# A cross-attention block in float32: half of the W1 product by seven block products, a re-ordered W2 sum, and the second norm's statistics at another place

## The chip, the cores and the metric

The kernel runs on one core of a Trainium2 chip. The metric is the device time of one execution in microseconds (us), lower is better. A core has a matrix engine (PE, whose weight loads are listed as PEld), a vector engine (DVE), an activation engine (ACT), a general engine (POOL) and a queue engine that issues transfers (SP). Each engine works through its own list of instructions in order, and they meet at semaphores.

## The reference

There are 128 batch rows of 128 tokens with 256 features; everything is float32.

```python
q = (x @ Wq + bq), k = (c @ Wk + bk), v = (c @ Wv + bv)       # 16 heads of 16 features
scores = einsum('bhqd,bhkd->bhqk', q, k) / 4
scores = where(j < i, scores, -1e30)                          # strictly earlier keys only
attn = softmax(scores); attn[:, :, 0, :] = 0
ctx = einsum('bhqk,bhkd->bhqd', attn, v)
x1 = layer_norm(x + ctx @ Wo + bo, g1, b1_ln)
out = layer_norm(x1 + relu(x1 @ W1 + b1) @ W2 + b2, g2, b2_ln)   # W1: 256 x 1024, W2: 1024 x 256
```

## The kernel before

Two batch rows at a time (a "pair", 256 tokens) go through the block; there are 64 pairs. The order of the instructions on every engine is written out by hand: the functions are called in the order in which the engines are to have the work, and no planner changes it. From pair 7 on, `step(p)` is the loop's body. It works on several pairs at once, each at another stage:

- pair p: scores (`scores_both`), mask, exponential, sums and normalisation, values, and the turn of the probabilities (`turn` on DVE, then `bring`, 16 transfers issued by SP);
- pair p + 1: queries and keys; pair p + 2: tokens transposed on DVE (`tokens`);
- pair p - 2: probabilities times values (`weigh`, `context`), output product, first sum, its statistics (`attention_stats`) and `norm1`;
- pair p - 3: `residual1` on POOL, and the W1 product with its Relu (`hidden`), eight feature blocks of 128 as float32 products of 128 x 128 weights and 256 tokens; the program's one product becomes two passes on PE;
- pair p - 4: the W2 product by seven block products (`second_by_seven`), with the combinations of the hidden tile formed on POOL (`combine_hidden`, a step's first POOL work) and of W2 once (`combine_w2`); the seven results, in two banks `py` and `pz`, are added to the residual `x1b` on DVE (`sum_of_seven`, lines L823 and L831), and the second norm's statistics follow at the step's end (`stats` on DVE, `scale_and_shift` on POOL);
- pair p - 5: `norm2` on ACT, `finish` on POOL, `store`.

The product by seven is the Winograd form: a 2 x 2 block product takes seven block products instead of eight, and more additions. Its sum in the kernel before, with t of four blocks:

```python
        add(t, x1b, 0)
        add(t[:, 1:], t[:, 1:], 1)
        add(t[:, 2:], t[:, 2:], 2)
        add(t[:, 1::2], t[:, 1::2], 3)
        nc.vector.tensor_tensor(
            t[:, :3], t[:, :3], pz[:, : 3 * P].rearrange("p (n d) -> p n d", d=P), ALU.add
        )
```

PE's order in a step is: L483/L493 (`weigh`), L376 (scores), L261 (queries), L512 (output product), L261 (keys), L301 (values), L794 (W2 by seven), L699 (W1). DVE's is: masks (L390, L743) and maxima (L747, L754), first sum (L538) and its statistics (L525, L526), softmax sums (L421, L422), turn of x1 (L663), tokens (L247), first probability turn (L436), `sum_of_seven`, two more turns (L436), the second norm's statistics (L525, L526). ACT has `context` (L505), the exponentials (L762), queries (L272), `norm1` (L554), keys (L291), values (L311, L316), `norm2` (L591) and the Relus (L707).

Every product's result lies in one of eight PSUM banks. The scores take banks 6, 7, 4, 5 (low half) and 0 to 3 (high half); queries 4, output product 5, keys 0, values 1, py 6, pz and the context product 7; the W1 product takes 2, 3, 4, 0. `empty(n)` puts n empty instructions into PE's list; `second_by_seven` has one behind each of its seven products, and pair 1's W1 product (`hidden`, outside the loop) has two or three behind each product.

Work tiles come from pools: a tile of the same tag takes the slot of an older one when that one's readers are done. `hT` and `hS` have one slot each, `t2` two.

Of the kernel before, what the change touches and what calls it, by code (L numbers as in the profile page):

```python
# [8 lines left out]
F32 = mybir.dt.float32  # L9
# [10 lines left out]
def tile_cross_attention_block(  # L20
# [104 lines left out]
    load_tokens(0, slice(0, 2))  # L125
    wk = weight(Wk, "wk")
    wq = weight(Wq, "wq")
    c_first = const.tile([P, 4, D], F32, tag="c_first", name="c_first")
    nc.scalar.dma_start(c_first[:, 0:2], c[0:2].rearrange("b p d -> p b d"))
    bk_c = column(bk, "bk_c")  # L130
    bq_c = column(bq, "bq_c")
# [78 lines left out]
    def at_bank(i, name):  # L210
        return psum.tile([P, 512], F32, tag=f"b{i}", name=name)
# [39 lines left out]
    def add_bo(p):  # L251
        st = states[p]
        st["xb"] = proj.tile([P, 2, D], F32, tag="xb", name=f"xb_{p}")
        nc.gpsimd.tensor_tensor(
            st["xb"], tokens_of[p // 2][:, p % 2 * 2 : p % 2 * 2 + 2], bov_r[:, None, :].to_broadcast([P, 2, D]), ALU.add
        )
# [47 lines left out]
                )  # L304

    def values_out(p):
        st = states[p]
        pv = st.pop("pv")
        st["vz"], st["vd"] = vzs[p % 2], vds[p % 2]
        for s in range(2):  # L310
            nc.scalar.copy(  # L311
                st["vz"][:, s, :, 0:4:3, :],
                pv[:, s * D : (s + 1) * D].rearrange("p (r e d) -> p r e d", e=2, d=DK),
            )
        for e in range(2):
# [69 lines left out]
    def mask(p, hi, rs):  # L385
        st = states[p]
        n = P if hi else HP
        no = neg.rearrange("p u j -> p (u j)") if hi else neg[:, 1, :]
        for r in rs:
            nc.vector.tensor_tensor(  # L390
                st["sm", hi][:, 4 * r : 4 * r + 4, :],
                st["sps", hi][r][:, : 4 * n].rearrange("p (n j) -> p n j", j=n),
                no[:, None, :].to_broadcast([P, 4, n]),
                ALU.add,
            )
# [185 lines left out]
    def scale_and_shift(p):  # L581

        st = states[p]
        deviation(p, 2)
        shift(p, 2)
# [199 lines left out]
    def second_by_seven(p):  # L785

        st = states[p]
        hT, hs = st["hT"], st["hS"]
        py = st["py"] = at_bank(6, f"py_{p}")
        pz = st["pz"] = at_bank(7, f"pz_{p}")  # L790

        def product(out, left, right, after):
            for k in range(FC // 2):
                nc.tensor.matmul(  # L794
                    out, left(k), right(k), start=(k == 0), stop=(k == FC // 2 - 1)
                )
                empty(after // (FC // 2) + (after % (FC // 2) > k))

        def raw(e, s):
            return lambda k: hT[:, 2 * k + e, s * P : (s + 1) * P]  # L800

        def weights(e, h):
            return lambda k: w2[:, 2 * k + e, h * P : (h + 1) * P]

        product(py[:, :P], raw(0, 0), weights(0, 0), 1)
        product(pz[:, :P], raw(1, 0), weights(1, 0), 1)
        product(pz[:, 2 * P : 3 * P], raw(1, 1), lambda k: wt[:, 3, k], 1)
        product(py[:, 3 * P :], lambda k: hs[:, 0, k], lambda k: wt[:, 0, k], 1)
        product(py[:, 2 * P : 3 * P], lambda k: hs[:, 2, k], lambda k: wt[:, 2, k], 1)
        product(py[:, P : 2 * P], lambda k: hs[:, 1, k], lambda k: wt[:, 1, k], 1)  # L810
        product(pz[:, P : 2 * P], lambda k: hs[:, 3, k], weights(1, 1), 1)

    def sum_of_seven(p):

        st = states[p]
        t2 = st["t2"] = ffn.tile([P, 2, D], F32, tag="t2", name=f"t2_{p}")
        t = t2.rearrange("p s (h d) -> p (s h) d", h=2)
        py, pz = st.pop("py"), st.pop("pz")
        x1b = st.pop("x1b").rearrange("p s (h d) -> p (s h) d", h=2)

        def add(to, of, at):
            n = to.shape[1]
            nc.vector.tensor_tensor(  # L823
                to, of, py[:, None, at * P : (at + 1) * P].to_broadcast([P, n, P]), ALU.add
# [6 lines that stand above are left out]
        nc.vector.tensor_tensor(  # L831
            t[:, :3], t[:, :3], pz[:, : 3 * P].rearrange("p (n d) -> p n d", d=P), ALU.add
        )

    def second_half(p, s):

# [331 lines left out]
    def sixth(p):  # L1168

        weigh(p - 2)  # L1170
        context(p - 2)
        scores_both(p)
        add_bo(p - 1)
        mask(p, 0, B)
# [36 lines left out]

    def step(p):
        last = p == NP - 1
        weigh(p - 2)
        context(p - 2)
        scores_both(p)
        if p == 7:
            norm2(p - 6)
        combine_hidden(p - 4, POOL_ALONE)
        if p == 7:  # L1220
            finish(p - 6)
            store(p - 6)
        add_bo(p - 1)
        load_ahead(p)
        mask(p, 0, B)
        if last:
            mask(p, 0, A)
        mask_high(p, A)
        exponential_by_head(p, 1, ONES)
        mask_high(p, B)  # L1230
        exponential_by_head(p, 1, TWOS)
        if not last:
            mask(p, 0, A)
        low_maximum(p)
        exponential_by_head(p, 0, range(H))
        if not last:
# [134 lines left out]
```

## Time and profile before

| | us |
|---|---|
| median of three runs | 1527.93 (1526.05 to 1528.2) |
| the profiled execution | 1528.67 |
| its span in the profile | 1527.0 |
| PE busy | 1514.3 (99%) |
| DVE busy | 1332.4 (87%) |
| POOL busy | 1255.9 (82%) |
| ACT busy | 1118.3 (73%) |

The median and the profiled execution are whole device times; the span runs from the first to the last instruction that the profiler recorded. Times within the trace are us from the span's start. A group's row gives the busy time, the mean duration in ns, and the idle time of its engine just before it with what ended most of it; a timeline's row gives start, duration, engine, line, operation and, in brackets, the idle time before it. PE's idle time means little by itself, as its ends are modelled; starts are measured.

### The profile page before, as it was taken

How to read it: one execution, taken by the hardware profiler on the slowest of the kernel's cores; microseconds unless marked ns; L12 is line 12 of the kernel's file. 1: busy time of each engine (PE TensorE's matmuls, PEld its weight loads, DVE VectorE, ACT ScalarE, POOL GpSimd, SP SyncE). 2: the span in 40 equal slices, each digit the busy share in tenths (PEclk: the TensorE clock that was granted, in tenths of full speed). 3: DMA queues.
4: the chain of work that ended last, by engine and by line, in shares of the span. 5: the costliest groups of instructions: out<-in, count | busy, mean ns of one | idle time of the engine just before them, and what ended most of it. 6: DMA issues, size and time to landing. Idle time of an engine off the chain costs nothing.

```text
span 1527.0 us, 47892 instructions
## 1 busy us (share of the span) xinstructions
PE 1514.3 (99%) x17926; PEld 1360.6 (89%) x17926; DVE 1332.4 (87%) x2498; ACT 1118.3 (73%) x3391; POOL 1255.9 (82%) x1282
## 2 busy tenths in 40 slices
PE   8999999999999999999999999999999999999998
PEld 7788998998989989989989899899899898998997
DVE  7989988988988988889889889889898898898885
ACT  5668777877877877778778778777777787787752
POOL 6876988888888888888888888888888888888883
PEclk9999999999999999999999999999999999999999
DMA  9356665555656656655556666566566566564441
GB/s 192 87 120 141 154 156 132 135 136 132 143 139 138 143 120 141 148 132 135 137 134 142 145 134 136 132 136 148 134 136 138 128 141 147 133 144 109 115 112 49
DMA packets 415285, 204.24 MB, mean 134 GB/s; under 512 B 282448, under 2 KB 383056, under 8 KB 415056
## 3 DMA queue, kind: packets, MB, share of 16 engines
q1 hardware_dynamic: 412768, 199.34, 56.7%
q8 instruction: 144, 2.36, 0.7%
q10 hardware_dynamic: 2288, 1.85, 0.5%
q14 instruction: 85, 0.70, 0.2%
HBM read 70.26 MB, written 33.29 MB: 68 GB/s over the span
## 4 chain that ended last, share of the span: by engine, by line
PE 94%; DVE 3%; POOL 1%; DMA 1%; issue 1%; ACT 0%; SPq 0%; POOLq 0%; DVEq 0%
PE ph L699 28%; PE py L794 14%; PE pz L794 10%; PE pq L261 7%; PE po L512 7%; PE pv L301 7%; PE pk L261 7%; PE pss L376 6%; PE pc L493 4%; PE pc L483 2%; DVE tb L436 1%; PE py L719 0%; DMA x1t<-tbx 0%; DVE sm L390 0%; DVE su L421 0%
## 5 line engine op out<-in xcount | busy, mean ns | idle before, releaser
L699 PE MATMUL ph<-x1T,w 128*128 128x256 f32 x2048 | 453.6, 380 | 0.7 <-DMA x1T<-x1t 0.7
L699 PEld LDWEIGHTS ph<-x1T,w 128*128 128x128 f32 x2048 | 385.0, 190 | 50.9 <-issue 1.2
L423 POOL TENSOR_TENSOR sm<-sm,rs 128x1024 f32<-128x1024 f32 x192 | 359.3, 1898 | 3.9 <-DVE rs L422 3.3
L762 ACT ACTIVATE sm<-pss,nmx 128x128 f32<-128x128 f32 x944 | 249.9, 414 | 127.3 <-DMA pT<-tb 81.0
L707 ACT ACTIVATE hT<-ph,b1e_c 128x256 f32<-128x256 f32 x504 | 209.1, 467 | 171.3 <-PE ph L699 161.3
L762 ACT ACTIVATE sm<-sm,nmx 128x64 f32<-128x64 f32 x944 | 232.2, 337 | 5.1 <-DVE nmx L754 0.3
L421 DVE TENSOR_REDUCE su<-sm 128x8 f32<-128x1024 f32 (+1 forms) x192 | 225.8, 1176 | 4.0 <-ACT sm L409 3.8
L436 DVE STREAM_TRANSPOSE tb<-sm 128x1024 f32<-128x1024 f32 x186 | 221.0, 1214 | 0.0
L390 DVE TENSOR_TENSOR sm<-pss,neg 128x256 f32<-128x256 f32 (+1 forms) x276 | 108.2, 435 | 121.2 <-PE pss L376 115.4
L532 POOL TENSOR_SCALAR ve<-mv 128x2 f32<-128x2 f32 x127 | 28.7, 226 | 191.7 <-DVE mv L526 190.9
L794 PE MATMUL py<-wt,hS 128*128 128x128 f32 x1440 | 170.6, 275 | 0.0
L794 PEld LDWEIGHTS py<-wt,hS 128*128 128x128 f32 x1440 | 165.7, 192 | 0.0
L747 DVE TENSOR_REDUCE nmx<-pss 128x4 f32<-128x512 f32 x236 | 150.8, 680 | 0.0
L261 PE MATMUL pq<-xT,wq 128*128 128x256 f32 x504 | 125.5, 392 | 0.5 <-DVE sm L390 0.5
L291 ACT ACTIVATE kT<-pk,bkh,half 128x256 f32<-128x256 f32 x252 | 120.3, 558 | 4.0 <-PE pk L261 4.0
L512 PE MATMUL po<-wo,cxT 128*128 128x256 f32 x512 | 121.3, 380 | 0.7 <-ACT cxT L505 0.7
L301 PE MATMUL pv<-wv,cT 128*128 128x256 f32 x512 | 121.0, 380 | 0.0
L261 PE MATMUL pk<-cT,wk 128*128 128x256 f32 x504 | 119.2, 380 | 0.0
L512 PEld LDWEIGHTS po<-wo,cxT 128*128 128x128 f32 x512 | 97.1, 190 | 14.3 <-ACT cxT L505 1.2
L261 PEld LDWEIGHTS pq<-xT,wq 128*128 128x128 f32 x504 | 90.9, 190 | 20.8 <-issue 9.6
L301 PEld LDWEIGHTS pv<-wv,cT 128*128 128x128 f32 x512 | 97.4, 190 | 13.0
L261 PEld LDWEIGHTS pk<-cT,wk 128*128 128x128 f32 x504 | 95.9, 190 | 13.0 <-issue 0.2
(135 smaller groups left out, 2966.6 us busy)
## 6 DMA issues: line engine op xcount, KB each, us to landing
pT<-tb SPq DMA_DIRECT2D x976, 96.0 KB
x1t<-tbx SPq DMA_DIRECT2D x252, 64.0 KB
x1T<-x1t SPq DMA_DIRECT2D x63, 256.0 KB
out_dram<-t SPq DMA_DIRECT2D x63, 256.0 KB
xb<-in_x_dram SPq DMA_DIRECT2D x124, 128.0 KB
cb<-in_ctx_dram SPq DMA_DIRECT2D x124, 128.0 KB
x<-in_x_dram SPq DMA_DIRECT2D x31, 512.0 KB
w<-in_L_xattn_W_dram SPq DMA_DIRECT2D x2, 1024.0 KB
```

What stands on the lines that cost most here:

```text
L261: nc.tensor.matmul(ps[:, m * TP : (m + 1) * TP], w[:, k, m * P : (m + 1) * P], src[:, k, :], start=(k == 0), stop=(k == KC - 1),)
L291: nc.scalar.activation(st["kT"][:, m, e, :], pk[:, m * TP : (m + 1) * TP], AF.Identity, bias=bkh[:, m, e : e + 1], scale=half[:, e : e + 1],)
L301: nc.tensor.matmul(pv[:, s * D : (s + 1) * D], st["cT"][:, k, s * P : (s + 1) * P], wv[:, k, :], start=(k == 0), stop=(k == KC - 1),)
L421: nc.vector.tensor_reduce(su, sm[:, part, :], AX.X, ALU.add)
L423: nc.gpsimd.tensor_tensor(sm[:, part, :], sm[:, part, :], rs[:, :, None].to_broadcast([P, part.stop - part.start, n]), ALU.mult,)
L436: nc.vector.transpose(st["tb"][:, :, at : at + 256].rearrange("p j (n a) -> p n j a", a=32), st["sm", hi].rearrange("p h j -> p (h j)")[:, ...
L512: nc.tensor.matmul(po[:, s * D : (s + 1) * D], cxT[:, k, s, :], wo[:, k, :], start=(k == 0), stop=(k == KC - 1),)
L699: nc.tensor.matmul(ph[:, i * TP : (i + 1) * TP].rearrange("p (s i a) -> p s i a", s=2, a=32), w1[:, k, (f + i) * P : (f + i + 1) * P], st[ ...
L707: nc.scalar.activation(st["hT"][:, f + i, :], ph[:, i * TP : (i + 1) * TP], AF.Relu, bias=(b1e_c if p else b1_c)[:, f + i : f + i + 1], sc ...
L747: nc.vector.tensor_reduce(st["nmx", 1][:, 4 * r : 4 * r + 4], st["sps", 1][r].rearrange("p (n j) -> p n j", j=P), AX.X, ALU.max, negate=True,)
L762: nc.scalar.activation(sm[:, h, :], src, AF.Exp, bias=nmx[:, h : h + 1], scale=1.0)
L794: nc.tensor.matmul(out, left(k), right(k), start=(k == 0), stop=(k == FC // 2 - 1))
```

## The change

Blocks 0 to 3 of the eight W1 feature blocks are formed as two 2 x 2 block products (NI = 2) by seven products each; blocks 4 to 7 stay as they were, one bank each. The combinations of W1 are formed once on POOL (`combine_w1`, in `sixth`), those of x1 in each step on POOL (`combine_normed`), and the seven results are put together in the hidden tile: one copy on ACT (`keep`), five adds on DVE (`u2`, `u3`, `rest`), and then a Relu from SBUF to SBUF. The W2 sum becomes one copy on ACT (`keep_first`) and six adds on DVE (`sum_of_products`). The second norm's statistics of a pair move from the end of its step to behind `low_maximum` of the next step, and `norm2` moves to behind `rest`. Each of the first six W2 products gets 7 empty instructions for 1, the last 6: 48 in a step for 7. The first context tile gives its own storage up and shares the slots of the context blocks. `sum_of_seven` and `hidden` stay in use behind the loop.

```diff
-    c_first = const.tile([P, 4, D], F32, tag="c_first", name="c_first")
+    c_first = loads.tile([P, 4, D], F32, tag="cb2", name="c_first", bufs=2)
...
-        product(py[:, :P], raw(0, 0), weights(0, 0), 1)
+        product(py[:, :P], raw(0, 0), weights(0, 0), 7)
...
+    def combine_normed(p):
+        st = states[p]
+        x1T = st["x1T"]
+        xs = st["xS"] = ffn.tile([P, 4, NS, 32], F32, tag="xS", name=f"xS_{p}", bufs=1)
+        nc.gpsimd.tensor_tensor(xs[:, 0], x1T[:, 1, :, 0, :], x1T[:, 1, :, 1, :], ALU.add)
+        nc.gpsimd.tensor_tensor(xs[:, 2], x1T[:, 0, :, 0, :], x1T[:, 1, :, 0, :], ALU.subtract)
+        nc.gpsimd.tensor_tensor(xs[:, 1], xs[:, 0], x1T[:, 0, :, 0, :], ALU.subtract)
+        nc.gpsimd.tensor_tensor(xs[:, 3], x1T[:, 0, :, 1, :], xs[:, 1], ALU.subtract)
+
+    class Hidden:
+        WHERE = {1: (2, 0), 6: (2, 1), 7: (3, 0), 4: (3, 1), 2: (4, 0), 3: (4, 1), 5: (5, 0)}
...
+        def run(self, which):
...
+            ps = self.of(which)
+            for i in range(NI):
+                nc.tensor.matmul(
+                    ps[:, i * P : (i + 1) * P].rearrange("p (n a) -> p n a", a=32),
+                    left(i), right, start=True, stop=True,
+                )
+        def keep(self):
+            nc.scalar.copy(self.h[:, 0, 0], self.one(1))
+        def u2(self):
+            nc.vector.tensor_tensor(self.h[:, 1, 0], self.h[:, 0, 0], self.one(6), ALU.add)
+        def u3(self):
+            nc.vector.tensor_tensor(self.h[:, 1, 1], self.h[:, 1, 0], self.one(7), ALU.add)
+            nc.vector.tensor_tensor(self.h[:, 0, 1], self.h[:, 1, 1], self.one(4), ALU.add)
+        def rest(self):
+            odd = self.hT[:, 1 : 2 * NI : 2].rearrange("p i (s t) -> p i s t", s=2)
+            nc.vector.tensor_tensor(
+                odd, odd, self.one(5)[:, :, None, :].to_broadcast([P, NI, 2, P]), ALU.add
+            )
+            low = self.h[:, :, 0]
+            nc.vector.tensor_tensor(
+                low, low, self.of(2, 2).rearrange("p (e i t) -> p e i t", e=2, i=NI), ALU.add
+            )
+        def relu(self, f):
+            nc.scalar.activation(
+                self.hT[:, f], self.plains.get(f, self.hT[:, f]), AF.Relu,
+                bias=b1e_c[:, f : f + 1], scale=1.0,
+            )
...
+    def sum_of_products(p):
...
+        add(u[:, 1], u[:, 0], py[:, P : 2 * P])
+        add(u[:, 2], u[:, 1], py[:, 2 * P : 3 * P])
+        add(t[:, :3], x1b[:, :3], u)
+        add(t[:, 3], x1b[:, 3], u[:, 2])
+        add(t[:, 1::2], t[:, 1::2], py[:, None, 3 * P :].to_broadcast([P, 2, P]))
+        add(t[:, :3], t[:, :3], pz[:, : 3 * P].rearrange("p (n d) -> p n d", d=P))
...
         low_maximum(p)
+        if p > 7:
+            second_stats(p - 5)
         exponential_by_head(p, 0, range(H))
...
         values(p)
-        values_out(p)
-        norm2(p - 5)
...
         second_by_seven(p - 4)
-        hidden(p - 3, range(FC))
+        spread_values(p)
+        keep_first(p - 4)
+        h = Hidden(p - 3)
+        h.run(1)
+        h.run(6)
+        h.keep()
+        stack_values(p)
...
         turn(p, 1, 0)
-        sum_of_seven(p - 4)
+        sum_of_products(p - 4)
+        h.u2()
+        h.run(7)
+        h.run(4)
+        h.u3()
+        h.run(2)
+        h.run(3)
+        h.run(5)
+        h.rest()
+        norm2(p - 5)
+        h.plain([4], 1)
+        h.relu(4)
+        h.plain([5], 0)
+        h.relu(5)
+        h.plain([6], 2)
+        h.relu(6)
         turn(p, 1, 1)
+        h.plain([7], 1)
+        h.relu(7)
+        for f in range(2 * NI):
+            h.relu(f)
         turn(p, 0, 0)
...
         finish(p - 5)
         store(p - 5)
-        stats(p - 4, states[p - 4]["t2"], 2)
-        scale_and_shift(p - 4)
+        if last:
+            second_stats(p - 4)
```

More of the change, by code (lines that the diff above doesn't have):

```diff
@@ L306, in values_out, with spread_values @@
     def values_out(p):
+        spread_values(p)
+        stack_values(p)
+    def spread_values(p):
         st = states[p]
-        pv = st.pop("pv")
+        pv = st["pv"]
         st["vz"], st["vd"] = vzs[p % 2], vds[p % 2]
@@ L314, in values_out, with stack_values @@
             )
+    def stack_values(p):
+        st = states[p]
+        pv = st.pop("pv")
         for e in range(2):
@@ L803, in weights @@
             return lambda k: w2[:, 2 * k + e, h * P : (h + 1) * P]
-        product(py[:, :P], raw(0, 0), weights(0, 0), 1)
[L806 to L811, printed above, removed]
+        product(py[:, :P], raw(0, 0), weights(0, 0), 7)
+        product(pz[:, :P], raw(1, 0), weights(1, 0), 7)
+        product(pz[:, 2 * P : 3 * P], raw(1, 1), lambda k: wt[:, 3, k], 7)
+        product(py[:, 3 * P :], lambda k: hs[:, 0, k], lambda k: wt[:, 0, k], 7)
+        product(py[:, 2 * P : 3 * P], lambda k: hs[:, 2, k], lambda k: wt[:, 2, k], 7)
+        product(py[:, P : 2 * P], lambda k: hs[:, 1, k], lambda k: wt[:, 1, k], 7)
+        product(pz[:, P : 2 * P], lambda k: hs[:, 3, k], weights(1, 1), 6)
     def sum_of_seven(p):
@@ L833, in sum_of_seven, with combine_w1 @@
         )
+    NI = 2
+    w1t = const.tile([P, 4, NI, P], F32, tag="w1t", name="w1t")
+    def combine_w1():
+        w = w1.rearrange("p k (i e f) -> p k e i f", e=2, f=P)[:, :, :, :NI]
+        nc.gpsimd.tensor_tensor(w1t[:, 0], w[:, 0, 1], w[:, 0, 0], ALU.subtract)
+        nc.gpsimd.tensor_tensor(w1t[:, 1], w[:, 1, 1], w1t[:, 0], ALU.subtract)
+        nc.gpsimd.tensor_tensor(w1t[:, 2], w[:, 1, 1], w[:, 0, 1], ALU.subtract)
+        nc.gpsimd.tensor_tensor(w1t[:, 3], w[:, 1, 0], w1t[:, 1], ALU.subtract)
@@ new lines, in combine_normed @@
+    def combine_normed(p):
+        st = states[p]
+        x1T = st["x1T"]
[4 more added lines that the diff above has]
+        nc.gpsimd.tensor_tensor(xs[:, 3], x1T[:, 0, :, 1, :], xs[:, 1], ALU.subtract)
@@ new lines, in tile_cross_attention_block, with __init__, of, one @@
+    class Hidden:
+        WHERE = {1: (2, 0), 6: (2, 1), 7: (3, 0), 4: (3, 1), 2: (4, 0), 3: (4, 1), 5: (5, 0)}
+        def __init__(self, p):
+            st = states[p]
+            self.p, self.x1T, self.xs = p, st["x1T"], st["xS"]
+            self.hT = st["hT"] = ffn.tile([P, FC, TP], F32, tag="hT", name=f"hT_{p}", bufs=1)
+            self.h = self.hT[:, : 2 * NI].rearrange("p (i e) (s t) -> p e s i t", e=2, s=2)
+            self.banks, self.plains = {}, {}
+        def of(self, which, n=1):
+            at, n0 = self.WHERE[which]
+            if at not in self.banks:
+                self.banks[at] = at_bank(at, f"phs_{self.p}_{at}")
+            return self.banks[at][:, n0 * NI * P : (n0 + n) * NI * P]
+        def run(self, which):
+            raw = lambda s, k: self.x1T[:, s, :, k, :]
+            given = lambda k, e: lambda i: w1[:, k, (2 * i + e) * P : (2 * i + e + 1) * P]
+            xs, ws = lambda i: self.xs[:, i], lambda n: (lambda i: w1t[:, n, i])
+            right, left = {
+                1: (raw(0, 0), given(0, 0)), 2: (raw(0, 1), given(1, 0)),
+                3: (xs(3), given(1, 1)), 4: (raw(1, 1), ws(3)),
+                5: (xs(0), ws(0)), 6: (xs(1), ws(1)), 7: (xs(2), ws(2)),
+            }[which]
+            ps = self.of(which)
[4 more added lines that the diff above has]
+                )
+        def one(self, which):
+            return self.of(which).rearrange("p (i t) -> p i t", i=NI)
+        def keep(self):
[19 more added lines that the diff above has]
+            )
+        def plain(self, fs, at):
+            ps = at_bank(at, f"ph_{self.p}_{fs[0]}")
+            for i, f in enumerate(fs):
+                self.plains[f] = ps[:, i * TP : (i + 1) * TP]
+                for k in range(KC):
+                    nc.tensor.matmul(
+                        self.plains[f].rearrange("p (s i a) -> p s i a", s=2, a=32),
+                        w1[:, k, f * P : (f + 1) * P], self.x1T[:, :, :, k, :],
+                        start=(k == 0), stop=(k == KC - 1),
+                    )
@@ new lines, in keep_first, with add @@
+    def keep_first(p):
+        u = states[p]["u"] = ffn.tile([P, 3, P], F32, tag="u", name=f"u_{p}", bufs=1)
+        nc.scalar.copy(u[:, 0], states[p]["py"][:, :P])
+    def sum_of_products(p):
+        st = states[p]
+        t2 = st["t2"] = ffn.tile([P, 2, D], F32, tag="t2", name=f"t2_{p}")
+        t = t2.rearrange("p s (h d) -> p (s h) d", h=2)
+        py, pz, u = st.pop("py"), st.pop("pz"), st.pop("u")
+        x1b = st.pop("x1b").rearrange("p s (h d) -> p (s h) d", h=2)
+        def add(to, one, two):
+            nc.vector.tensor_tensor(to, one, two, ALU.add)
+        add(u[:, 1], u[:, 0], py[:, P : 2 * P])
[4 more added lines that the diff above has]
+        add(t[:, :3], t[:, :3], pz[:, : 3 * P].rearrange("p (n d) -> p n d", d=P))
@@ L1173, in sixth @@
         add_bo(p - 1)
+        combine_w1()
         mask(p, 0, B)
@@ L1223, in step @@
         add_bo(p - 1)
+        combine_normed(p - 3)
         load_ahead(p)
@@ L1253, in step @@
         second_by_seven(p - 4)
-        hidden(p - 3, range(FC))
+        spread_values(p)
+        keep_first(p - 4)
[3 more added lines that the diff above has]
+        h.keep()
+        stack_values(p)
         if p + 2 < NP:
@@ L1264, in step, with second_stats @@
         store(p - 5)
-        stats(p - 4, states[p - 4]["t2"], 2)
-        scale_and_shift(p - 4)
+        if last:
+            second_stats(p - 4)
+    def second_stats(p):
+        stats(p, states[p]["t2"], 2)
+        scale_and_shift(p)
     third()
```

## The prediction

> **What bounds the kernel now.** I read the page first (busy shares, then the chain that ended last), then the list of waits, then PE's and DVE's timelines over one step, because a kernel in which one engine is busy throughout can still have a second one close behind it.
>
> ```profile
> PE 1514.3 (99%) x17926; PEld 1360.6 (89%) x17926; DVE 1332.4 (87%) x2498; ACT 1118.3 (73%) x3391; POOL 1255.9 (82%) x1282
> PE 94%; DVE 3%; POOL 1%; DMA 1%; issue 1%; ACT 0%; SPq 0%; POOLq 0%; DVEq 0%
> PE ph L699 28%; PE py L794 14%; PE pz L794 10%; PE pq L261 7%; PE po L512 7%; PE pv L301 7%; PE pk L261 7%; PE pss L376 6%; PE pc L493 4%; PE pc L483 2%; DVE tb L436 1%; PE py L719 0%; DMA x1t<-tbx 0%; DVE sm L390 0%; DVE su L421 0%
> ```
>
> PE sets the time, and the largest piece of the chain is the W1 product (L699), half of which the change reworks. The steady loop, one pass of `step` for each pair of batch rows, shows in the windows view from the first mask of one step to the first mask 52 steps later (us, then busy time of PE, PEld, DVE, ACT, POOL); 1211.24 / 52 = 23.29 us a step:
>
> ```profile
> 192.64:1403.88 1211.24, 1211.24 (x14576) 1096.73 (x14565) 1074.26 (x2028) 922.22 (x2860) 1021.20 (x1041) 1.00 0.59 137
> ```
>
> The clock in that row is 1.00: no throttle. DVE is second, and its timeline over one step (start, duration, idle before) tells how far behind it is:
>
> ```profile
> 705.02 0.76 DVE L390 TENSOR_TENSOR sm<-pss,neg 128x256 f32<-128x256 f32 x2 [2.11 <-PE pss L376]
> 705.69 0.75 DVE L743 TENSOR_TENSOR pss<-pss,neg 128x256 f32<-128x256 f32 x2
> ...
> 718.93 1.20 DVE L436 STREAM_TRANSPOSE tb<-sm 128x1024 f32<-128x1024 f32 x1
> 720.06 0.65 DVE L823 TENSOR_TENSOR t<-x1b,py 128x512 f32<-128x512 f32 x1
> 720.74 1.46 DVE L823 TENSOR_TENSOR t<-t,py 128x384 f32<-128x384 f32 x3
> 722.31 0.56 DVE L831 TENSOR_TENSOR t<-t,pz 128x384 f32<-128x384 f32 x1
> 722.78 2.36 DVE L436 STREAM_TRANSPOSE tb<-sm 128x1024 f32<-128x1024 f32 x2
> 725.07 0.38 DVE L525 BATCH_NORM_STATS2 bs<-t 128x6 f32<-128x256 f32 x1
> ...
> 726.02 0.18 DVE L526 BATCH_NORM_AGGREGATE mv<-bs 128x2 f32<-128x6 f32 x1
> 728.31 0.42 DVE L390 TENSOR_TENSOR sm<-pss,neg 128x256 f32<-128x256 f32 x1 [2.11 <-PE pss L376]
> ```
>
> DVE idles once a step, for PE's scores, and nowhere else. A following instruction that needs no result of the one before starts some 0.08 us before that one's recorded end (L390's pair takes 0.67 from start to start, 0.42 each), so DVE could have gone on at 726.02 + 0.18 - 0.08 = 726.12: its spare time is 728.31 - 726.12 = 2.19 us, its work 21.10 us a step. The list of waits has the same stall over the whole run, 2.02 us in each of 57 steps:
>
> ```profile
> DVE sm L390 <- PE pss L376: 115.4, 57, 3.2
> ```
>
> So two numbers decide: what PE saves, and whether DVE's new work stays under 2.19 us.
>
> **PE's part.** One step's timeline (x counts passes; each float32 product of the program is two):
>
> ```profile
> 711.05 1.89 PE L301 MATMUL pv<-wv,cT 128*128 128x256 f32 x8
> 712.78 1.05 PE L794 MATMUL py<-w,hT 128*128 128x128 f32 x8
> ...
> 718.13 1.06 PE L794 MATMUL pz<-w,hS 128*128 128x128 f32 x8
> 719.03 7.07 PE L699 MATMUL ph<-x1T,w 128*128 128x256 f32 x32
> 726.03 0.43 PE L483 MATMUL pc<-pT,vd 128*32 128x64 f32 x16
> ```
>
> A pass of 256 columns goes every (712.78 - 711.05) / 8 = 0.216 us, and the W1 product is 32 of them. The W2 product, already by seven, is 56 passes of 128 columns in 6.25 us: 0.112 each. Removed: 4 feature blocks, 16 passes, 3.46 us. Added: 7 products x 2 blocks x 2 passes = 28 passes, 3.13 us. PE saves 0.33 us a step: 22.96. Against that saving speaks the Trainium skill, "TensorE: Matmul & The Clock Gate", section "Back-to-back issue gap": with its weight load a matmul of 128 columns takes about 81 ns where the columns alone take 56. By an estimate from these two figures the 28 passes would take 28 x 0.112 x 81/56 = 4.5 us, and PE would lose 1.1 a step. The rows decide against it: 0.112 and 0.216 are 1 to 1.93, weight loads included.
>
> The empty instructions grow from 7 to 48 a step. Behind L794's groups there is one each now, and they cost nothing (0.112 across the groups' borders). The nearest row for many is pair 1's W1 product, where two or three stand behind each product, 44 in all:
>
> ```profile
> 79.51 7.14 PE L699 MATMUL ph<-x1T,w 128*128 128x256 f32 x32 [0.67 <-DMA x1T<-x1t]
> ```
>
> Its 32 passes take 7.14 against 7.07 above, so 44 cost at most 0.07. I take nothing for the 41; a gain from them has no row that shows one either.
>
> **DVE's part.** Prices, from groups by shape (busy, mean ns):
>
> ```profile
> L823 DVE TENSOR_TENSOR t<-t,py 128x256 f32<-128x256 f32 x120 | 50.5, 421 | 4.1
> L538 DVE TENSOR_TENSOR t<-po,xb 128x512 f32<-128x512 f32 x64 | 43.5, 680 | 10.9 <-PE po L512 10.9
> L823 DVE TENSOR_TENSOR t<-t,py 128x384 f32<-128x384 f32 x60 | 33.3, 555 | 2.1
> ```
>
> ```profile
> L831 DVEq EVENT_SEMAPHORE  x58: 21/21/21, 165.5 to 1509.1; - x58
> ```
>
> 128 more elements cost 0.134, so an add of 128 is 0.287. How the next one stands to it adds or takes away: needs nothing of it, -0.083; needs its result, +0.034 (720.06 + 0.65 to 720.74); needs its result and waits on PE's semaphore too, +0.104 (720.74 + 1.46 = 722.20 to 722.31: L831, whose products PE had finished at 719.2, spends a queued wait on the second semaphore, the last row).
> - Removed, `sum_of_seven`: 722.78 - 720.06 = 2.72.
> - Added, `sum_of_products`: two adds of 128, 0.32 each; the 384 add, 0.47; a 128 add, 0.32; a 256 add before the two-semaphore add, 0.525; the last 384, 0.47. Sum 2.43: shorter by 0.29 only, since it is six instructions for five.
> - Added, five adds on the hidden product: `u2` 0.525 (before the two-semaphore `u3`), `u3` 0.455 and 0.525, `rest` with 512 elements twice, 0.714 and 0.60. Sum 2.82.
> - `second_stats`, 726.12 - 725.07 = 1.05, moves from the end of the step to behind the low maximum: the same work.
>
> Net +2.53 (bounds: 2.3, if the three second semaphores that it adds cost nothing; 2.7, if two more of the eleven adds pay one). It exceeds 2.19: DVE needs 21.10 + 2.53 = 23.63 a step and becomes the bound, 0.34 over today's 23.29, and PE's saving turns into waiting.
>
> **What else moves, and its cover.** The moved statistics wait for nothing new; behind them on DVE queue attention's sum and softmax sums, 1.05 later within the step, and ACT's exponentials come the earlier for it. The tail of POOL's step loses that chain. POOL's four `combine_normed` adds of 128 elements (under 1.27 each, by the row below for 512; by length about 0.4) go into its idle 2.42 us:
>
> ```profile
> 709.62 1.27 POOL L254 TENSOR_TENSOR xb<-x,bov_r 128x512 f32<-128x512 f32 x1
> 713.31 0.23 POOL L532 TENSOR_SCALAR ve<-mv 128x2 f32<-128x2 f32 x1 [2.42 <-DVE mv L526]
> ```
>
> POOL is busy 1021.20 / 52 = 19.6 us a step, so even with 1.6 more it stays under 23. ACT gets two copies, `keep_first` and `keep`, and its last four Relus wait for `rest` and then read and write SBUF, as L591 does:
>
> ```profile
> 718.77 0.64 ACT L311 COPY vz<-pv 128x256 f32<-128x256 f32 x2
> 720.07 1.09 ACT L591 ACTIVATE t<-t,nb,sd 128x256 f32<-128x256 f32 x2
> ```
>
> That is at most 0.64 and about 0.5 a Relu, 2.0 behind `rest`. With 922.22 / 52 = 17.7 busy ACT has room, but `context` then ends about when the next masks start, and the last scores need its bank: PE, 23.63 - 22.96 = 0.67 ahead by then, covers that. PE's block 6 reuses the bank that `u2` reads: `u2` is done 720.06 - 705.02 + 1.05 + 2.43 + 0.42 = 18.9 us after the mask, then come 8 passes, 1.7, and 728.31 - 726.03 = 2.3 until the next mask may start: 22.9, under 23.63. `norm2` later on ACT delays finish and store, which SP issues behind 16 transfers anyway. `c_first` shares the slots of context blocks long before the loop, `combine_w1` is four POOL adds once: both zero, at most 2 us once.
>
> **The sum.** Intervals of steps 8 to 61 are DVE's: 54 x 0.34 = +18.4. Steps 7 (statistics not moved in) and 62 (without 1.2 us of token transposes) are PE's: -0.7. The last step holds two statistics, and there PE waits:
>
> ```profile
> 1450.46 0.76 DVE L390 TENSOR_TENSOR sm<-pss,neg 128x256 f32<-128x256 f32 x2 [3.21 <-PE pss L376]
> ...
> 1464.82 0.65 DVE L823 TENSOR_TENSOR t<-x1b,py 128x512 f32<-128x512 f32 x1
> ```
>
> ```profile
> 1469.56 1.16 PE L794 MATMUL py<-w,hT 128*128 128x128 f32 x8
> ```
>
> There the sum starts 14.36 + 1.05 = 15.4 after the mask, `rest` ends 2.43 + 2.82 + 0.1 later, 20.75, and four Relus put the next W2 product at 22.6, where it now starts at 1469.56 - 1450.46 = 19.1: +3.5 (1 to 4). Together +21.2 on the profiled execution's 1528.67 (span 1527.0): 1549.9. The median of the runs is 0.7 lower: 1549.
>
> **Rivals.**
> - *Faster: chained adds overlap.* If adds that need each other's results started as early as independent ones, both blocks would cost 4.1, not 5.25, net +1.4, inside the 2.19; PE stays the bound at 22.96: 57 x -0.33 = -19, about 1510 with a tail of +1. It decides where DVE's net falls under 1.86. The Trainium skill's "VectorE: DVE Perf Modes", section "The DRAIN you can't avoid", says that a semaphore between chained operations costs nothing extra, which would be this case. The row against it: 0.68 from L823's start to the next's where it needs the result, 0.65 long, and 0.08 overlap in L390's pair. Chance, with every other way into faster: 0.12.
> - *Even.* The second semaphore is free and the 512 adds go at 0.65: net 2.2 to 2.3, so +0 to +6 over 54 steps, and a tail of 1 to 3: 1529 to 1537. Chance 0.12, 0.05 of it within the 0.2% (3.1 us) that a measurement can tell from no change.
> - *Slower still.* ACT's late Relus hold `context`, the scores and with them DVE's masks: 0.2 a step more, 54 x 0.2 = +11: 1560. It decides from about 0.63 for a Relu from SBUF, where the scores end 0.7 later. Chance 0.12.
> - *My forecast*, DVE-bound, 1538 to 1556: 0.64.
>
> Range 1531 to 1562: faster, the low end of even and what lies beyond *slower still* leave out 0.2. Faster 0.12, same 0.05, slower 0.83.
>
> **What would show it.** DVE's idle before L390's successor gone (from 115 us to a few), DVE busy 95% or more; the step at 23.6; the new 28 passes at 0.112; PE idle some 0.6 a step, before the queries or before block 6. I am wrong if DVE still waits for scores in each step, or if PE shows gaps at the empty instructions.

## The result, and the profile after

The changed kernel takes 1623.65 us (median of four runs, 1617.44 to 1633.11) against 1528.07 for the kernel before beside it: 1.0633 times as long, with an interval of 1.058 to 1.0686. The prediction had 1549, with a range up to 1562. The side was right, the size was not: the profiled execution rose by 1617.44 - 1528.67 = 88.8 us where the sum said 21.2.

The page after, in the same order as before: busy shares, then the chain that ended last by engine and by line.

```profile
PE 1536.8 (95%) x18610; PEld 1369.0 (85%) x18610; DVE 1519.0 (94%) x2840; ACT 1168.2 (72%) x3505; POOL 1377.2 (85%) x1514
DVE 56%; PE 30%; SPq 4%; POOL 3%; issue 3%; DMA 2%; ACT 1%; DVEq 0%; ACTq 0%; POOLq 0%
DVE t L950 9%; DVE su L429 9%; PE ph L931 7%; DVE nmx L755 6%; DVE tb L444 5%; PE pss L384 5%; SPq L459 4%; DVE bs L533 4%; DVE pss L751 3%; DVE sm L398 3%; DVE nmx L762 3%; PE pc L501 3%; PE py L802 2%; PE ph L707 2%; DVE tbx L671 2%
```

The chain has moved from PE (94% before) to DVE, and its first line is L950, the new sum. The waits after (total us, times, longest) say the same from the other side: DVE's stall for the scores, 115.4 us before, is down to 2.8, and PE now waits for `u2` (L904) in each of 57 steps.

```profile
PEld ph L931 <- DVE hT L904: 86.7, 57, 3.3
PE ph L931 <- DVE hT L904: 63.8, 57, 2.9
DVE sm L398 <- PE pss L384: 2.8, 3, 1.1
```

The windows view over 50 steps, first mask to first mask (PE, PEld, DVE, ACT, POOL busy), for the kernel before and for the changed one:

```profile
192.64:1357.30 1164.66, 1164.66 (x14016) 1054.55 (x14005) 1032.93 (x1951) 886.75 (x2750) 981.94 (x1001) 1.00 0.60 137
```

```profile
199.49:1434.63 1235.14, 1181.55 (x14609) 1059.78 (x14600) 1194.46 (x2252) 930.43 (x2851) 1086.81 (x1201) 1.00 0.57 130
```

That is 23.29 and 24.70 us a step (24.63 in most, the rest 24.8 to 25.8). So 70.5 of the 88.4 us of span lie in these 50 steps, 6.9 ahead of them and 11.1 behind. The prediction had 23.63 a step: 1.07 too little, 53.5 of the 88.4 - 21.2 = 67.2 us that it missed. DVE's timeline over the second half of a step shows where (start, duration, idle before):

```profile
708.71 0.57 DVE L950 TENSOR_TENSOR u<-u,py 128x128 f32<-128x128 f32 x2
709.31 1.83 DVE L950 TENSOR_TENSOR t<-x1b,u 128x384 f32<-128x384 f32 x2
711.18 0.42 DVE L950 TENSOR_TENSOR t<-t,py 128x256 f32<-128x256 f32 x1
711.71 0.55 DVE L950 TENSOR_TENSOR t<-t,pz 128x384 f32<-128x384 f32 x1
712.18 0.41 DVE L904 TENSOR_TENSOR hT<-hT,phs 128x256 f32<-128x256 f32 x1
...
715.01 2.36 DVE L444 STREAM_TRANSPOSE tb<-sm 128x1024 f32<-128x1024 f32 x2
```

The five hidden adds take 715.01 - 712.18 = 2.83 us; the prediction had 2.82. The six adds of `sum_of_products` take 712.18 - 708.71 = 3.47; the prediction had 2.43. The whole difference is in the row of 709.31, the two adds of `x1b` and `u`, whose inputs both lie in SBUF: 711.18 - 709.31 = 1.87 instead of 0.47 + 0.32. By shape (busy, mean ns), it is above all the shorter one:

```profile
L950 DVE TENSOR_TENSOR t<-x1b,u 128x128 f32<-128x128 f32 x57 | 77.4, 1357 | 0.0
L950 DVE TENSOR_TENSOR t<-x1b,u 128x384 f32<-128x384 f32 x57 | 37.6, 660 | 1.9
```

An add of 128 elements that lasts twice as long as one of 384 isn't paying for its length. POOL's timeline at the same time:

```profile
705.65 3.76 POOL L431 TENSOR_TENSOR sm<-sm,rs 128x1024 f32<-128x1024 f32 x2
709.36 1.64 POOL L574 TENSOR_TENSOR x1b<-x,g_r 128x512 f32<-128x512 f32 x1
711.08 1.27 POOL L577 TENSOR_TENSOR x1b<-x1b,be1b_r 128x512 f32<-128x512 f32 x1
```

L574, the multiply of `residual1`, takes 1.64 where the one like it behind it takes 1.27, and ends at 711.00; the 128 add (some 709.79 to 711.14) ends 0.14 later. It looks as if each had waited for the other in turn. The experiments test that.

### The profile page after: what moved, and what is told of

Same layout as the page of the kernel before. It is cut to its first block, busy times and chain, and to the rows that moved or that the text cites. A ratio compares the mean times of both kernels' runs of the same rounds, so it can differ in the third digit from the quotient of the medians.

```text
span 1615.4 us, 52589 instructions
## 1 busy us (share of the span) xinstructions
PE 1536.8 (95%) x18610; PEld 1369.0 (85%) x18610; DVE 1519.0 (94%) x2840; ACT 1168.2 (72%) x3505; POOL 1377.2 (85%) x1514
## 4 chain that ended last, share of the span: by engine, by line
DVE 56%; PE 30%; SPq 4%; POOL 3%; issue 3%; DMA 2%; ACT 1%; DVEq 0%; ACTq 0%; POOLq 0%
DVE t L950 9%; DVE su L429 9%; PE ph L931 7%; DVE nmx L755 6%; DVE tb L444 5%; PE pss L384 5%; SPq L459 4%; DVE bs L533 4%; DVE pss L751 3%; DVE sm L398 3%; DVE nmx L762 3%; PE pc L501 3%; PE py L802 2%; PE ph L707 2%; DVE tbx L671 2%
## 5 line engine op out<-in xcount | busy, mean ns | idle before, releaser
L431 POOL TENSOR_TENSOR sm<-sm,rs 128x1024 f32<-128x1024 f32 x192 | 359.6, 1900 | 3.6 <-DVE rs L430 3.3
L931 PE MATMUL ph<-x1T,w 128*128 128x256 f32 x912 | 223.6, 388 | 64.9 <-DVE hT L904 63.8
L931 PEld LDWEIGHTS ph<-x1T,w 128*128 128x128 f32 x912 | 165.4, 191 | 106.0 <-DVE hT L904 86.7
L921 ACT ACTIVATE hT<-ph,b1e_c 128x256 f32<-128x256 f32 x228 | 108.2, 474 | 199.5 <-PE ph L931 199.4
L788 POOL TENSOR_TENSOR hS<-hT 128x512 f32<-128x512 f32 x57 | 72.7, 1276 | 119.3 <-ACT hT L921 119.3
L384 PE MATMUL pss<-kT,qT 32*64 32x256 f32 (+1 forms) x3840 | 120.4, 332 | 0.5 <-ACT hT L715 0.4
L950 DVE TENSOR_TENSOR t<-x1b,u 128x384 f32<-128x384 f32 x114 | 110.4, 1009 | 1.9
L384 PEld LDWEIGHTS pss<-kT,qT 32*64 32x64 f32 x3840 | 88.3, 131 | 24.0 <-ACT cxT L513 14.1
```

The lines of the kernel that those rows point to most:

```text
L384: nc.tensor.matmul(st["sps", hi][r][s * HP : (s + 1) * HP, m * 2 * n : (m + 1) * 2 * n].rearrange("p (e j) -> p e j", e=2), st["qT"][strip ...
L431: nc.gpsimd.tensor_tensor(sm[:, part, :], sm[:, part, :], rs[:, :, None].to_broadcast([P, part.stop - part.start, n]), ALU.mult,)
L931: nc.tensor.matmul(self.plains[f].rearrange("p (s i a) -> p s i a", s=2, a=32), w1[:, k, f * P : (f + 1) * P], self.x1T[:, :, :, k, :], st ...
L950: nc.vector.tensor_tensor(to, one, two, ALU.add)
```

## The experiments

The theory: a DVE add with both inputs in SBUF and a POOL instruction that reads SBUF exclude each other, and the one that comes second waits until the other has ended. The main rival: the new sum is slow in itself (its chain, its tiles, its place), whatever POOL does.

**e1: the changed kernel with the old sum.**

```diff
-        keep_first(p - 4)
...
-        sum_of_products(p - 4)
+        sum_of_seven(p - 4)
```

> The changed kernel with the old sum of the W2 product (every add has one input in PSUM) in place of the copy and the six adds; the W1 product by seven, the moved statistics and the empty instructions stay. Port theory (an add of DVE with both inputs in SBUF waits for a POOL instruction that is reading SBUF): DVE's work per step falls from 24.63 by the sum's 3.62 and rises by 2.72, so 23.73 a step and a span of 1527 + 54 x 0.44 + about 6 = 1557, DVE still without idle time. Rival (the step is not set by DVE's instructions but by PE waiting for the hidden product's second add, whatever the sum costs): 24.6 a step, 1617.

Measured: 1584.43 us, ratio 1.0376 (1.0361 to 1.0392), most steps 24.20. DVE's and POOL's timeline:

```profile
792.66 0.65 DVE L831 TENSOR_TENSOR t<-x1b,py 128x512 f32<-128x512 f32 x1
792.97 1.28 POOL L574 TENSOR_TENSOR x1b<-x,g_r 128x512 f32<-128x512 f32 x1
793.35 1.46 DVE L831 TENSOR_TENSOR t<-t,py 128x384 f32<-128x384 f32 x3
794.92 0.55 DVE L839 TENSOR_TENSOR t<-t,pz 128x384 f32<-128x384 f32 x1
795.39 0.42 DVE L904 TENSOR_TENSOR hT<-hT,phs 128x256 f32<-128x256 f32 x1
```

The old sum, one input of each add in PSUM, runs under the same POOL multiplies in 795.39 - 792.66 = 2.73, as before, and L574 takes its 1.28. So the "shorter" sum costs 39 of the 95.6 us. My expectation was 0.47 a step too low (23.73). It took a difference of 0.90 between the sums, the mean of a window with irregular steps, where the usual step has 3.47 - 2.73 = 0.74. It also left out that the first mask now starts 0.18 later behind the last transpose than in the changed kernel, and that the reciprocal and transpose ahead of the tokens (L430, L671) take 0.1 more.

**e2: the changed kernel, with `residual1` behind `finish` and `norm2` behind the second plain block's Relu.**

```diff
-        residual1(p - 3)
         second_by_seven(p - 4)
...
-        norm2(p - 5)
         h.plain([4], 1)
         h.relu(4)
         h.plain([5], 0)
         h.relu(5)
+        norm2(p - 5)
...
         store(p - 5)
+        residual1(p - 3)
```

> The changed kernel, its sum as it is, but POOL has nothing to do while the sum runs: the residual goes behind finish, and norm2 on ACT, for which finish waits, behind the second plain Relu. All arithmetic stays. Port theory: the 128-element add from SBUF falls from 1.36 to 0.29 and the 384-element one from 0.67 to about 0.56; the step is 24.63 - 1.07 - 0.12 = 23.44, the span about 1527 + 54 x 0.15 + 6 = 1541. Rival (the add is slow by itself: its place in the tile, the block of the residual that it reads again): it stays at 1.36, the step at 24.63, the span at 1615.

Measured: 1620.18 us, ratio 1.0617 (1.0599 to 1.0634). The time missed the expectation, because POOL wasn't quiet: the last softmax multiply (L431) was still running.

```profile
830.55 3.76 POOL L431 TENSOR_TENSOR sm<-sm,rs 128x1024 f32<-128x1024 f32 x2
833.22 1.71 DVE L950 TENSOR_TENSOR t<-x1b,u 128x384 f32<-128x384 f32 x2
```

L431 ends at 834.31. Now it is the 384 add that is long, 1511 ns in the mean, and the 128 add behind it takes 278, with the same tiles and the same place as its 1357 in the changed kernel. That speaks against the rival: slow is whichever add meets a POOL instruction.

**e3: the kernel before with the shorter sum alone** (`keep_first` behind `second_by_seven`, `sum_of_products` for `sum_of_seven`).

> The kernel before with one part of the change alone, the shorter sum (copy on ACT, six adds on DVE). Port theory: POOL is at the residual at that time here too, so one of the two adds from SBUF takes about 1.3; DVE's work rises by 0.9 to 22.0, DVE still waits about 1.3 a step for PE, and the time is that of before, 1528. Rival (the adds cost what their length says, and the slow one in the changed kernel comes from its surroundings there): DVE waits 2.5 a step, the time is 1528 as well.

Measured in one run: 1588.99 us, 24.39 a step, where both readings had 1528. In nearly every step both adds met a POOL instruction (L569, then L597) and took 1.44 and 1.35 us in the mean. A second cost showed too: the copy `keep_first` stands on ACT behind `norm2`, and DVE waits 1.2 us a step for it (the last row).

```profile
819.85 1.27 POOL L569 TENSOR_TENSOR x1b<-x1b,be1b_r 128x512 f32<-128x512 f32 x1
820.05 2.75 DVE L848 TENSOR_TENSOR t<-x1b,u 128x384 f32<-128x384 f32 x2
821.08 1.58 POOL L597 TENSOR_TENSOR t<-t,g_r 128x512 f32<-128x512 f32 x1
```

```profile
DVE u L848 <- ACT u L837: 69.1, 56, 2.3
```

So the shorter sum alone, placed so, costs some 60 us.

**e4: the kernel before with three more 128-element adds a step, into an unused tile**: one with a PSUM input and one with two SBUF inputs ahead of the sum, one with two SBUF inputs behind attention's sum.

```diff
+    def probe_sbuf(p):
+        nc.vector.tensor_tensor(probe[:, 0], ident, be1_r[:, :P], ALU.add)
+
+    def probe_psum(p):
+        nc.vector.tensor_tensor(probe[:, 1], ident, states[p]["py"][:, :P], ALU.add)
+
+    def probe_idle(p):
+        nc.vector.tensor_tensor(probe[:, 2], ident, be1_r[:, :P], ALU.add)
...
         attention_sum(p - 2)
+        probe_idle(p)
...
         turn(p, 1, 0)
+        probe_psum(p - 4)
+        probe_sbuf(p)
         sum_of_seven(p - 4)
```

> The kernel before with three extra adds of 128 elements a step on DVE, which write a tile that nobody reads: one with both inputs in SBUF and one with an input in PSUM, both just before the sum, where POOL is busy, and one with both inputs in SBUF just after the attention sum, where POOL waits for DVE. Port theory: 0.6 to 1.4 for the first (it waits for the rest of a POOL instruction of 1.9 or 1.3), 0.29 for the second, 0.29 for the third. Rival (length alone sets the price): 0.29 for all. The time stays at 1528 in both, since DVE has 2.19 to spare.

Measured in one run: 1530.05 us; the step stays 23.29, since PE is still the bound. The prices are 250 ns with a PSUM input, while the same POOL multiply (L423) runs, and 282 with two SBUF inputs while POOL waits. The rows give the shortest, the median and the longest; the 1049 belongs to one of three steps in which POOL was running after all.

```profile
L1218 DVE TENSOR_TENSOR probe<-ident,py x57: 247/250/251, 161.2 to 1464.5; 128x128 f32<-128x128 f32 x57
L1221 DVE TENSOR_TENSOR probe<-ident,be_r x57: 281/282/1049, 152.2 to 1457.2; 128x128 f32<-128x128 f32 x57
```

With two SBUF inputs beside POOL it is this, in two steps:

```profile
625.24 1.91 POOL L423 TENSOR_TENSOR sm<-sm,rs 128x1024 f32<-128x1024 f32 x1
626.86 0.43 DVE L1215 TENSOR_TENSOR probe<-ident,be_r 128x128 f32<-128x128 f32 x1
...
695.37 1.90 POOL L423 TENSOR_TENSOR sm<-sm,rs 128x1024 f32<-128x1024 f32 x1
696.74 0.68 DVE L1215 TENSOR_TENSOR probe<-ident,be_r 128x128 f32<-128x128 f32 x1
```

L423 ends at 627.15 and 697.27, the adds at 627.29 and 697.42: 0.14 and 0.15 behind it, as in the changed kernel. My expected size was too high for the median (425) only because the multiply usually had 0.28 us left.

**e11: e1 with one such add, placed where POOL's multiply has just begun.**

```diff
         add(t, x1b, 0)
+        if probe is not None:
+            nc.vector.tensor_tensor(probe, ident, be1b_r[:, :P], ALU.add)
         add(t[:, 1:], t[:, 1:], 1)
```

> e1 (the changed kernel with the sum from PSUM) with one 128-element add of two SBUF constants into an unused tile behind the sum's first add, where GpSimd's residual1 multiply has just begun; an idle VectorE does such an add in 0.28 us. Theory (it ends 0.14 us after the running GpSimd instruction does): it starts 0.25 us into a multiply of 1.27, so it takes 1.1 to 1.2 us, the step grows by 0.8 to 1.0 and the time to 1627 to 1640. Rival (the slow adds of the changed kernel are slow for their own operands, the tiles t, u and x1b): 0.28 to 0.45 us, the step grows by at most 0.4, the time 1590 to 1605.

Measured in one run: 1639.99 us, 25.17 a step where e1 has 24.23.

```profile
818.99 1.27 POOL L574 TENSOR_TENSOR x1b<-x,g_r 128x512 f32<-128x512 f32 x1
819.24 1.16 DVE L837 TENSOR_TENSOR probe<-ident,be1b_r 128x128 f32<-128x128 f32 x1
```

POOL ends at 820.26, the add at 820.40. Adding two constants into a tile that nobody reads, begun 0.25 us into POOL's multiply, costs 56 us. The rule holds to a few ns: an add of 128 elements with both inputs in SBUF ends 145 to 151 ns (nine cases in ten) behind the POOL instruction that it found running, whether that had 0.27 or 1.5 us left (e3, e4, e11 and the changed kernel); one of 384 ends 413 to 416 ns behind it (e2, e3). That is 0.14 less than the adds take alone, 0.28 and 0.56. So a POOL instruction with under 0.1 us left costs nothing itself: in the changed kernel 50 of the 57 adds of 384 start with 0.09 to 0.1 of L431 left and take their 557 ns. The next POOL instruction can still get ahead: two adds that start with 0.07 and 0.08 left lose to L574 behind it, take 1.72 us and end 0.41 behind that one.

**e6: e2 with the third softmax multiply of each step left out**, so that the low half's probabilities stay undivided.

> The changed kernel, with residual1 behind finish and norm2 behind the second plain block's Relu as in e2, and with the third of GpSimd's softmax multiplies in each step left out (the low half's probabilities stay undivided), so that GpSimd has no instruction running while the two adds with both inputs in SBUF run. Theory (such an add waits until GpSimd's running instruction ends): the 384 add takes 0.55 to 0.58 instead of 1.48, the 128 add stays at 0.28, the shorter sum is 2.4 to 2.5 us from start to start, the step 23.6 to 23.8, the time 1556 to 1572. Rival (the shorter sum is slow for another reason, its chain or its place behind the scores' transposes): a step of 24.4 to 24.6 as in e2, 1610 to 1620.

Measured: 1606.05 us, ratio 1.0513 (1.0497 to 1.0528). The add is cured (557 ns, and 284 for the 128 add), the time isn't: by its place `residual1` now holds POOL into the next step, the first norm comes late, and DVE stands some 0.85 us a step ahead of the turn of x1.

```profile
DVE tbx L673 <- ACT x L564: 51.6, 58, 2.5
```

**e9: e6 with `norm2` already behind the first plain block's Relu**, which takes that wait away.

> As e6 (the third softmax multiply of each step left out, residual1 behind finish), but with norm2 already behind the first plain block's Relu, so that GpSimd is done earlier and the first norm of the next step does not wait for it. Theory (in e6 the shorter sum took 2.43 us, as the prediction had it, and the step stayed long for the 0.83 us that VectorE waited for the first norm): that wait falls to under 0.1, VectorE's work is 23.7, the step 23.7 to 23.9, the time 1556 to 1572. Rival (VectorE's other work or TensorE's wait for u2 holds the step anyway): 24.2 or more, 1585 to 1606.

Measured: 1567.93 us, ratio 1.0253 (1.0239 to 1.0267), the steps 23.7 and 24.0 in turn.

```profile
DVE tbx L673 <- ACT x L564: 13.7, 30, 2.5
```

```profile
807.83 0.57 DVE L952 TENSOR_TENSOR u<-u,py 128x128 f32<-128x128 f32 x2
808.43 0.76 DVE L952 TENSOR_TENSOR t<-x1b,u 128x384 f32<-128x384 f32 x2
809.23 0.42 DVE L952 TENSOR_TENSOR t<-t,py 128x256 f32<-128x256 f32 x1
809.76 0.55 DVE L952 TENSOR_TENSOR t<-t,pz 128x384 f32<-128x384 f32 x1
810.23 0.41 DVE L906 TENSOR_TENSOR hT<-hT,phs 128x256 f32<-128x256 f32 x1
```

With POOL idle the six adds take 810.23 - 807.83 = 2.40 us; the prediction had 2.43. The steps of 24.0 are those in which DVE still stands 0.3 us ahead of the turn of x1 (the 30 waits above); why only every second step does, the runs don't show.

**e5, e10, e12: two feature blocks by seven products instead of four, with the old sum.** The hidden adds shrink with their length; e10 gives the plain blocks banks that no hidden add reads and goes back to one empty instruction behind each W2 product; e12 exchanges the first two of these banks.

```diff
-    NI = 2
+    NI = 1
...
-        h.plain([4], 1)
+        h.plain([2, 3], 0)
...
+        h.plain([4, 5], 1)
...
+        h.plain([6, 7], 5)
```

(The banks are e12's; e10 has 1 and 0, and e5 takes bank 5 for blocks 2 and 3 and leaves the others.)

> The changed kernel with two edits: the W2 product's sum as before (its inputs from PSUM), and only two of the eight feature blocks of W1 by seven products instead of four. Theory (VectorE's sum of durations sets the step): the five hidden adds shrink with their length from 2.86 to about 2.03 us (128 elements 0.42, 0.32 and 0.39; 256 elements 0.56 and 0.34), VectorE's work goes from 24.06 to 23.2, TensorE's from 22.96 to 23.13; with 0.1 to 0.15 of wait at the mask the step is 23.2 to 23.4, the time 1525 to 1540. Rival (the cost is not the adds' length but the five instructions, the new order of the step or the waits between engines, which stay): 24.0 or more a step, 1570 to 1585.

> As e5 (two feature blocks by seven products, the sum from PSUM), with the plain blocks in banks that no hidden add reads (2 and 3 in bank 1, 4 and 5 in bank 0, 6 and 7 in bank 5), and one empty TensorE instruction behind each product of W2 instead of seven. Theory (in e5 TensorE's 0.5 us of wait for u2 before block 6 made the step 23.45, and VectorE's work is 23.14): the wait is gone, VectorE and TensorE (23.13) limit together, 23.15 to 23.35 a step, the time 1522 to 1535. Rival (the wait is for VectorE's masks and returns elsewhere): 23.4 to 23.5, 1538 to 1546.

> As e10, with banks 0 and 1 of the plain blocks exchanged: the first plain blocks (2 and 3) no longer go to the bank that ScalarE's copies of the values have just read. Theory (in e10 the first passes behind the seven products start 0.09 and 0.10 us late because that bank was still being read): TensorE loses at most half of these 0.2 us, the step is 23.1 to 23.25 and the time 1526 to 1535, level with the kernel before. Rival (the change from passes of 128 to passes of 256 columns costs it, or VectorE's masks hold the step): 23.3, 1537 to 1542. No version with fewer blocks by seven products is then ahead of the kernel before by more than what VectorE leaves, 0.1 us a step.

Measured: e5 1545.92 us, ratio 1.0116 (1.0101 to 1.0131), most steps 23.45; e10 1539.9, 1.008 (1.0066 to 1.0094), 23.32; e12 1528.35, 1.0004 (0.9994 to 1.0013), 23.13. The times of e5 and e10 lie above what was expected, e10's step within it. Each was held by one bank. In e5 block 6 waits for `u2`; in e10 the first plain block waits for the values' second copy on ACT:

```profile
770.71 0.74 ACT L324 COPY vd<-pv 64x256 f32<-64x256 f32 x2
...
771.50 1.99 PE L931 MATMUL ph<-x1T,w 128*128 128x256 f32 x8
```

The copies end at 771.45, PE starts 0.05 later; with its operands alone it would have started at 771.40. In e12 the usual step is 23.13, PE's 23.29 less 0.16 that 14 passes of 0.112 save against 8 of 0.216. So the product by seven does save what its passes say, where DVE has room for its adds; but one step in ten of e12 is 0.8 to 1.2 longer (PE stands inside the scores' passes, see e8), the last step and what follows take 78.5 us where the kernel before takes 76.5, and the medians are level. No version ahead of the kernel before came out.

**e7: the kernel before with only the second norm's statistics moved.**

> The kernel before with only the second norm's statistics moved behind the low maximum. Theory (VectorE has the work either way, and its idle 2.19 us stay): TensorE stays the bound, the step at 23.29, the time 1525 to 1530. Rival (attention's sum and the softmax sums, 1.05 us later, are waited for by a transpose and through it by the context): up to 0.5 a step more, 1535 to 1555.

Measured: 1528.96 us, ratio 1.0006 (0.9996 to 1.0016); 23.29 a step. The move is free.

**e8: the kernel before with 48 empty instructions a step instead of 7.**

> The kernel before with only the empty TensorE instructions raised from 7 to 48 a step. The prediction took nothing for them: a step of 23.29, 1524 to 1530. Rival (each holds TensorE's sequencer for some tens of ns where TensorE is the bound): 41 x 0.02 = 0.8 a step, 1570.

Measured: 1534.1 us, ratio 1.0043 (1.0027 to 1.0058). That is above the expected 1524 to 1530. The usual step stays 23.29, as the prediction had it, but 6 of 50 are longer, by 0.65 to 1.38, together the 6 us that the time grew. In five of them PE stands inside the scores' passes, in the sixth inside the queries', and the waits name no engine:

```profile
754.01 0.65 PE L376 MATMUL pss<-kT,qT 32*64 32x128 f32 x11 [0.42 <-issue]
```

The list of DMA queues points at a cause. A queue that it calls "instruction" brings nine more packets than in the kernel before (first row; packets, MB, share of the span of 16 DMA engines):

```profile
q8 instruction: 144, 2.36, 0.7%
q8 instruction: 153, 2.51, 0.7%
```

In all six steps PE goes on 1.3 to 1.4 us after such a packet has ended, by the trace's records of single packets. The long steps of e12 and e10 end in the same way, after 1.4 to 1.5 us. It looks as if PE waits there for its own instructions; no run tests that.

## Why the prediction was right in its side and wrong in its size

**Right: PE's part.** PE's timeline in the changed kernel:

```profile
706.63 0.61 PE L892 MATMUL phs<-x1T,w 128*128 128x128 f32 x4
...
709.76 1.89 PE L931 MATMUL ph<-x1T,w 128*128 128x256 f32 x8
712.65 1.99 PE L931 MATMUL ph<-x1T,w 128*128 128x256 f32 x8 [1.00 <-DVE hT L904]
```

The 28 new passes take 709.76 - 706.63 = 3.13 us, the number predicted. By the Trainium skill's "TensorE: Matmul & The Clock Gate", section "Back-to-back issue gap", the estimate was 4.5; the trace disagrees for these passes. PE waits before block 6, the place that was named, 1.00 us a step instead of 0.6, because DVE is later. The 41 empty instructions, taken at nothing, aren't free where PE is the bound (e8: 6 us); in the steady steps of the changed kernel PE has no such stop among the scores' passes.

**Right: the bound moves to DVE, and the hidden adds cost 2.83 (2.82).** The *faster* rival needed chained adds that overlap; they don't. The statistics' move costs nothing (e7). The rivals *even* and *slower still* didn't come either: DVE's masks waited for nothing (2.8 us in all).

**Wrong: the price of `sum_of_products`.** The failed step is the line "the 384 add, 0.47; a 128 add, 0.32". The row behind it, L823's 384 elements at 555 ns, has one input in PSUM; the two new adds have `x1b` and `u`, both in SBUF. Alone they cost what was predicted (e9: 2.40 for the six against 2.43), beside POOL they cost the rest of its instruction: 1.87 instead of 0.79, 1.08 a step, and 3.47 + 21.10 - 2.72 + 2.82 = 24.67 is the step that was measured, 24.63. In the two steps of 25.8 both adds lost, to L574 and to L577 in turn. More or fewer such steps could make the scatter of the runs (1617 to 1633); only one run was traced.

```profile
783.21 2.99 DVE L950 TENSOR_TENSOR t<-x1b,u 128x384 f32<-128x384 f32 x2
783.25 1.27 POOL L574 TENSOR_TENSOR x1b<-x,g_r 128x512 f32<-128x512 f32 x1
784.59 1.46 POOL L577 TENSOR_TENSOR x1b<-x1b,be1b_r 128x512 f32<-128x512 f32 x1
```

This is a rule of the Trainium skill that the prediction passed over: "SBUF — State Buffer", section "Who interferes with whom", has a DVE instruction with two SBUF inputs contend with a GpSimd instruction that reads SBUF, for a port pair that the two engines share; the pair is locked for a whole instruction, and the second to come blocks. A DVE instruction with at most one SBUF input, outside the modes that use both ports, doesn't contend. The runs agree in both halves: 1357 ns against 285 (e9) with two SBUF inputs; with one, 250 (e4) and an unchanged sum of 2.73 (e1). The prediction looked at POOL's load as a sum (19.6 of 23 us busy) and asked whether it fits, not what POOL executes while the new adds run.

**Wrong, for the most part by the same step: the start and the tail.** Ahead of the window of 50 steps the prediction had nothing, a gain and a loss of 0.3; it is 199.49 - 192.64 = 6.85. In e1 that window begins at 195.22, so 4.3 of it go with the new sum. The other 2.6 were not split further; in the first step of the loop DVE waits 2.5 for the first norm, where the kernel before waits 0.7. In the last step the sum takes 4.53 instead of 2.43, both adds losing, and PE stands 2.88 before block 6: from the last first mask (1533.11) to the end 82.3 us against 76.5, +5.8 where the prediction had 3.5.

```profile
1548.03 0.57 DVE L950 TENSOR_TENSOR u<-u,py 128x128 f32<-128x128 f32 x2
1548.63 2.90 DVE L950 TENSOR_TENSOR t<-x1b,u 128x384 f32<-128x384 f32 x2
...
1552.56 0.41 DVE L904 TENSOR_TENSOR hT<-hT,phs 128x256 f32<-128x256 f32 x1
```

## What to carry to other kernels

Price an operation from a row with its shape and also with its operands' memories: the same add cost 0.28 us, or up to 1.67 (e4), by where its second input lay and what another engine was doing at that moment. Before moving VectorE inputs from PSUM to SBUF, lay GpSimd's timeline beside VectorE's at that place: an add with both inputs in SBUF that starts early in a GpSimd instruction paid for all the rest of it, however short the add. And when two engines are within 10% of each other, a saving on the one is worth only what the other has spare: here 0.33 us a step on PE was bought with 2.8 on DVE, which had 2.19 to spare.

## What the runs showed of the hardware that was not expected

- A VectorE add with both inputs in SBUF ends a fixed time behind the GpSimd instruction that it found running with 0.27 us or more left: 145 to 151 ns for 128 elements, 414 for 384. With under 0.1 us left it lost nothing, unless the next GpSimd instruction got ahead of it. The GpSimd instruction that comes second pays too: 1.64 instead of 1.27 us (L574 in the changed kernel).
- 41 more empty TensorE instructions a step left the usual step at 23.29 us, but 6 of 50 steps grew by up to 1.4 us; ratio 1.0043. Each of these stops ended 1.3 to 1.4 us behind a packet of the DMA queue listed as "instruction"; that TensorE waited for that packet isn't tested.
